# Regrouping the score blocks and the attends of a two-layer graph network into clusters, with one rotation of eight PSUM banks

## The chip, the cores and the metric

The kernel runs on one core of a Trainium2 chip. The metric is the device time of one launch in microseconds (us); lower is better. Three runs of the kernel before gave 2311.16, 2311.50 and 2311.74 us, a median of 2311.5 us. One more execution was taken with the hardware profiler; all durations below come from it.

The engines are called PE (TensorE, matrix products), ACT (ScalarE), DVE (VectorE), POOL (GpSimd) and SP (SyncE, which here only issues DMAs). Each works through its own list of instructions in order and waits on semaphores where it needs another engine's result.

## The reference

All data are float32: x is 64 x 256 x 512, adj is 64 x 256 x 256 with ones and zeros.

```python
# layer 0
feat_proj = feats @ fc_w.T + fc_b
logits = q + swapaxes(k, 2, 1)              # q, k: feat_proj times one row of weights each
masked = logits + (1.0 - adj_mat) * NEG_INF
masked = where(masked >= 0, masked, 0.01 * masked)
x1 = softmax(masked) @ feat_proj + feats
# layer 1: 8 heads of 64
Q, K, V = x1 @ W_q + b_q, x1 @ W_k + b_k, x1 @ W_v + b_v
scores = Q @ K.T / sqrt(64) + a[:, :, None] + c[:, None, :] + log(adj + 1e-9)
out = softmax(scores) @ V + x1
```

## The kernel before, in words

The 64 graphs are taken in 32 groups of two. One **step** of the program works on several groups at once: on group f the end of layer 0 and the projections of layer 1, on group a (one older) its attention, on group d (two older) the rest of its output, and on group n (one newer) the loading and the weights of layer 0. The function `step` (L1107) and `attention_and_layer_0` (L1068) write out by hand the order in which the pieces are issued: `A("scores:0")` issues `scores(0)` of group a, `F("pf.p1")` piece p1 of the product pf of group f, and so on. That order, cut to what belongs to one engine, is the order of each engine. No scheduler changes it.

**Products.** The four 512 x 512 x 512 products of a group (pf: features of layer 0; pq, pk, pv: queries, keys, values) are Strassen-like: seven block products p1 to p7 of four matmuls each. A float32 matmul is two passes of PE, so a block product shows as eight records. Three PSUM banks are reused within a product: r takes p1, then p6, p5 and p3 are added onto it; r2 takes p7, then p4 is added. Between these additions others read the same bank: `keep` (L437) lets ACT copy r after p1, p6 and p5 to SBUF, and `sum` (L442) lets DVE add such a copy to r1 or r2 and write one quarter of the result (`sum_11` reads r2 between p7 and p4). An addition onto a bank must wait for the reader before it.

**Attention of group a.** Index u is 0 to 3: graph u // 2, head group u % 2. `scores(u)` (L847) computes two blocks, jc = 0 and 1; each is four matmuls with 64 rows (two heads side by side in the rows of PE, `par`, each into a bank of its own), and one ACT exp over the pair of banks, 128 x 1024. `factor(u, jc)` (L876, DVE) multiplies by the adjacency, `both(u)` (L884, DVE) adds the two blocks, `parts(u)` (L908, DVE: a transpose and a reduction) prepares the sums of the softmax, `totals` (L922, PE) adds them over partitions. `attend(gr)` (L888) multiplies by v for one graph: 16 matmuls of 64 columns, two side by side, then two ACT copies. `turn(gr)`, `divide(gr)`, `complete(gr)` (DVE) and `store(gr)` finish a graph.

PE thus works in three shapes: full (128 rows, 128 columns), 64 rows by 128 columns (scores) and 128 rows by 64 columns (attend, totals).

**Order within a step before.** The head: pv.p5 of the step before, scores 0, attend 1 (of group d), scores 1, pv.p3, pv.p4, then the mix of layer 0 (`y`, four groups of eight records) and pf.p1, p2, p6, p7, p5, p3. The middle: scores 2, attend 0, totals, scores 3, pf.p4. Then pq, pk and pv up to p5, with scores no more. On DVE the tail of the step is: four `keys` (dot products with x), pq.sum_00, a piece of xsum, pq.sum_11, `divide:0`, four `dot_q` (on the x of group n), pq.sum_10, `complete:0`, `parts:2`, pk.sum_11, `adjt`, pk.sum_00, two `dot_k`, pk.sum_10, two `dot_k`, `turn_residual:0`, `weights:0`, `weights:1`, pv.sum_00. The x of group n goes into the only buffer of that name, so its DMA (`load_x`, L541, issued by SP) starts when `keys` has read the old x.

**PSUM.** Four single banks (`ps`) and two pairs of banks (`psc`); scores, and pq.p7 with `scores = True`, use the pairs.

Of the kernel before, what the change touches and what calls it, by code (L numbers as in the profile page):

```python
# [10 lines left out]
F32 = mybir.dt.float32  # L11
# [6 lines left out]
P = 128  # L18
# [7 lines left out]
def kernel(  # L26
# [137 lines left out]
    def fast():  # L164
        main = ExitStack()
        with main:
# [4 lines left out]
            six = main.enter_context(tc.tile_pool(name="six", bufs=6))  # L171
            ps = main.enter_context(
                tc.tile_pool(name="ps", bufs=4, space=bass.MemoryType.PSUM)
            )
            psc = main.enter_context(
                tc.tile_pool(name="psc", bufs=2, space=bass.MemoryType.PSUM)
# [4 lines left out]

            def pair(name):
                return psc.tile([P, 2, 512], F32, tag="pair", name=name)
# [205 lines left out]
            class Product:  # L389
# [5 lines left out]
                scores = False  # L395

# [21 lines left out]
                def fresh(self, n, scores=False):  # L418
                    name = f"{self.name}_{n}"
                    dst = (pair(name)[:, 0] if scores else bank(name)).rearrange(  # L420
                        "p (m k) -> p m k", m=2
                    )
                    self.add(n, dst, True)
                    return dst
# [36 lines left out]
                def p7(self):  # L461
                    self.r2 = self.fresh(7, self.scores)
# [66 lines left out]
            class Group:  # L529
# [235 lines left out]
                def begin(self):  # L765

                    g = self.g

                    def to(dst):
                        return lambda o, k: block(dst, o, k)  # L770

                    def to_v(o, k):
                        return self.v[:, TPG * k : TPG * (k + 1), o * HALF : (o + 1) * HALF]


                    self.d = {}
# [8 lines left out]
                    self.pq.scores = True  # L785
                    self.pk = Product(f"pk_{g}", "k", b, to(self.kT), False)
# [60 lines left out]
                def scores(self, u):  # L847


                    g, (gr, hg) = self.g, divmod(u, 2)  # L850
                    if u == 0:
                        self.e, self.esum, self.oTs, self.sms1, self.osb = {}, {}, {}, {}, {}
                    for jc in range(TPG):
                        t = gr * TPG + jc
                        sc = pair(f"sc_{g}_{u}_{jc}").rearrange("p a (b i) -> p a b i", b=2)
                        for pr in range(2):
                            for par in range(2):
                                rows = slice(par * HD, (par + 1) * HD)
                                nc.tensor.matmul(  # L859
                                    sc[:, par, pr, :],  # L860
                                    lhsT=self.kT[rows, 2 * hg + pr, ts(t, P)],
                                    rhs=self.qT[rows, 2 * hg + pr, ts(gr, N)],
                                    start=True,
                                    stop=True,
                                )
                        if g == NG - 1 and u == 3:

                            if jc == 0:
                                last = one.tile([P, 2, 2, 2, N], F32, tag="x", name="e_last")
                            e = last[:, jc]  # L870
                        else:
                            e = six.tile([P, 2, 2, N], F32, tag="e", name=f"e_{g}_{u}_{jc}")
                        nc.scalar.activation(e, sc, AF.Exp, bias=self.c[:, t : t + 1], scale=SCALE)  # L873
                        self.e[u, jc] = e
# [9 lines left out]
                def both(self, u):  # L884
                    self.esum[u] = two.tile([P, 2, 2, N], F32, tag="es", name=f"es_{self.g}_{u}")
                    nc.vector.tensor_tensor(self.esum[u], self.e[u, 0], self.e[u, 1], ALU.add)  # L886
# [21 lines left out]
                def parts(self, u):  # L908
# [5 lines left out]
                    pool, tag = ((two, "osb"), (one, "e0"), (one, "e0"), (one, "adj"))[u]  # L914
                    turned = pool.tile([P, NC * N], F32, tag=tag, name=f"est_{g}_{u}")
# [6 lines left out]
                def totals(self, gr, dst):  # L922


                    half = NC * N // B // 2
                    for par in range(2):
                        nc.tensor.matmul(  # L927
                            dst[par * HD : (par + 1) * HD, :].rearrange("p (a m) -> p a m", a=2),
                            lhsT=every[:, 0:HD], rhs=self.part[:, :, par * half : (par + 1) * half],
                            start=True, stop=True, skip_group_check=True,  # L930
                        )
                    self.tot = dst

                def totals_1(self):
                    self.totals(1, bank(f"tot_{self.g}_1")[:, 0 : NC * N // B])

                def totals_0(self):
                    self.totals(0, bank(f"tot_{self.g}_0")[:, 0 : NC * N // B])

                def ratios(self, gr):  # L940
                    self.rs = recip1[:, self.g % NR, gr]
                    nc.vector.reciprocal(self.rs.rearrange("p m b -> p (m b)"), self.tot)

                def ratios_of_all(self):


                    self.rs = recip1[:, self.g % NR, 1]
# [39 lines left out]
                def turn(self, gr):  # L987

                    g = self.g
                    self.osb[gr] = two.tile([P, NC * N], F32, tag="osb", name=f"osb_{g}_{gr}")  # L990
# [27 lines left out]
                def complete(self, gr):  # L1018
                    nc.vector.tensor_tensor(self.osb[gr], self.osb[gr], self.xb[gr], ALU.add)
# [5 lines left out]
                def finish(self, gr):  # L1025
# [3 lines left out]
                    self.osb[gr] = two.tile([P, NC * N], F32, tag="osb", name=f"osb_{g}_{gr}")  # L1029
# [77 lines left out]
            def step(d, a, f, n, check):  # L1107
# [24 lines left out]
                A("factor:3:0 factor:3:1 both:3")  # L1132
# [18 lines left out]
                if n is None:  # L1151
                    A("attend:1 totals_1 ratios:1 turn:1 divide:1 complete:1 store:1")
                    F("residual:1 turn_residual:1")

                    F("pv.p2 scores:0 pv.p6 pv.sum_00 factor:0:0 factor:0:1 scores:1 both:0 pv.p7")
                    F("factor:1:0 factor:1:1 both:1 scores:2 pv.p5 sums_1:0 scores:3 pv.sum_11")
                    F("ratios_t:0 ratios_r:0 factor:2:0 factor:2:1 pv.p3 pv.p4 factor:3:0 pv.sum_10")
                    F("factor:3:1 attend:0 finish:0 sums_of_e:1 attend:1")
# [8 lines left out]
                F("pv.sum_00")  # L1167
                A("parts:3")
# [237 lines left out]
```

## Time and profile before

| what | value |
|---|---|
| median of three runs | 2311.5 us |
| span of the profiled execution | 2308.8 us |
| mean granted clock of PE in that execution | 0.997 |
| busy in the span: DVE | 2124.2 us (92%) |
| busy in the span: ACT | 1071.8 us (46%) |
| busy in the span: POOL | 121.9 us (5%) |
| one step of the middle of the run, from the first y to the next | 70.88 us |
| in such a step: PE, DVE, ACT busy | 70.88, 65.9, 33.4 us |

The span runs from the first to the last instruction that the profiler recorded; the runs' time is 2.7 us longer than the span at the median, which is what lies around it. The steps repeat: of 30 distances between the starts of `y` in successive steps 29 are 70.88 us and one is 70.95 us. So one step stands for nearly all of the time, and a change per step counts some 30 times.

In the time lines below each row gives the start in us, the time in us from the first record's start to the last one's end, the engine, the line of the program, the operation, output and inputs, shapes, and the number of records that were merged. What stands in square brackets is idle time of that engine just before, and what ended it. Records of PE overlap by about 0.16 us, since a matmul's end is later than the start of its successor; for PE the distance between starts is the time that a group takes.

### The profile page before, as it was taken

The numbers are of one execution on the slowest core, as the hardware profiler recorded it, in microseconds if no ns is written. First come the engines' busy times: TensorE is split into PE (matmuls) and PEld (weight loads), VectorE is DVE, ScalarE is ACT, GpSimd is POOL, SyncE is SP. The second block draws the span as 40 slices with busy tenths as digits, with TensorE's granted clock in tenths as the row PEclk, the third lists the DMA queues.
The fourth block names the chain that finished last, engine by engine and source line by source line (L and its number), as shares of the span: only waits on it lengthen the run. The fifth ranks groups of instructions, "written<-read, shape, count | busy, mean of one in ns | idle before, by whom it ended". The sixth has DMA issues, their size and how long they took to land.

```text
span 2308.8 us, 33613 instructions
## 1 busy us (share of the span) xinstructions
PE 2294.2 (99%) x12618; PEld 1905.2 (83%) x12618; DVE 2124.2 (92%) x3180; ACT 1071.8 (46%) x1865; POOL 121.9 (5%) x120
## 2 busy tenths in 40 slices
PE   9999999999999999999999999999999999999997
PEld 6888888888888888888888888888888888888885
DVE  6899999999999999999999999999999999999997
ACT  3544444454445444454444454444544445444443
POOL 0000000000000000000000000000000000000000
PEclk9999999999999999999999999999999999999999
DMA  4122332223322233232233232332222323223312
GB/s 133 46 61 73 78 76 66 70 61 85 79 73 61 61 78 78 74 68 61 69 78 83 60 75 63 79 78 74 64 60 74 78 73 70 65 64 81 84 46 38
DMA packets 517264, 163.84 MB, mean 71 GB/s; under 512 B 415188, under 2 KB 478696, under 8 KB 517096
## 3 DMA queue, kind: packets, MB, share of 16 engines
q1 hardware_dynamic: 514440, 160.32, 28.8%
q8 instruction: 102, 1.67, 0.3%
q10 hardware_dynamic: 2656, 1.31, 0.2%
q14 instruction: 66, 0.54, 0.1%
HBM read 95.43 MB, written 66.12 MB: 70 GB/s over the span
## 4 chain that ended last, share of the span: by engine, by line
PE 98%; DVE 1%; DMA 0%; ACT 0%; issue 0%; ACTq 0%; DVEq 0%
PE pv L412 17%; PE pq L412 17%; PE pf L412 16%; PE pk L412 16%; PE sc L859 11%; PE oT L899 10%; PE y L689 9%; PE fp L718 1%; DMA fc_nat<-in_L_gnn_fc_w_dram 0%; PE rc L637 0%; DVE osb L1034 0%; PE tot L927 0%; DVE osb L1040 0%; PE xTp L705 0%; DVE osb L1033 0%; DVE x L756 0%
## 5 line engine op out<-in xcount | busy, mean ns | idle before, releaser
L873 ACT ACTIVATE e<-sc,c 128x1024 f32<-128x1024 f32 x254 | 269.0, 1110 | 79.2 <-PE sc L859 77.6
L879 DVE TENSOR_TENSOR e<-e,am 128x1024 f32<-128x1024 f32 x254 | 297.7, 1213 | 0.4 <-ACT e L873 0.4
L859 PE MATMUL sc<-qT,kT 64*128 64x256 f32 x2048 | 255.8, 390 | 0.3 <-ACT e L873 0.3
L899 PE MATMUL oT<-e,v 128*64 128x256 f32 x2032 | 233.4, 382 | 0.0
L859 PEld LDWEIGHTS sc<-qT,kT 64*128 64x128 f32 x2048 | 187.3, 187 | 52.6 <-issue 32.7
L495 POOL TENSOR_TENSOR pf_s<-pf_s,x 128x512 f32<-128x512 f32 x93 | 118.4, 1273 | 2106.1 <-ACT pf_s L494 2038.8
L689 PE MATMUL y<-e,x 128*128 128x256 f32 x992 | 225.6, 381 | 0.0
L899 PEld LDWEIGHTS oT<-e,v 128*64 128x64 f32 x2032 | 140.2, 137 | 85.3 <-issue 10.7
L689 PEld LDWEIGHTS y<-e,x 128*128 128x128 f32 x992 | 186.4, 190 | 23.7
L432 ACT ACTIVATE pq_s<-pq,cols 128x256 f32<-128x256 f32 x192 | 80.5, 470 | 249.1 <-PE pq L412 249.1
L494 ACT ACTIVATE pf_s<-pf,recip 128x256 f32<-128x256 f32 x186 | 77.9, 470 | 197.6 <-PE pf L412 197.6
L917 DVE TENSOR_REDUCE part<-est 128x32 f32<-128x1024 f32 x124 | 151.3, 1220 | 4.3
L916 DVE STREAM_TRANSPOSE est<-es 128x1024 f32<-128x1024 f32 x124 | 152.2, 1227 | 0.0
L886 DVE TENSOR_TENSOR es<-e,e 128x1024 f32<-128x1024 f32 x126 | 149.3, 1205 | 1.1
L695 ACT COPY yT<-y 128x512 f32<-128x512 f32 x124 | 72.6, 585 | 131.7 <-PE y L689 130.9
L429 ACT COPY pk_s<-pk 128x512 f32<-128x512 f32 x96 | 56.3, 586 | 165.7 <-PE pk L412 159.0
L906 ACT COPY oTs<-oT 128x512 f32<-128x512 f32 x128 | 75.0, 586 | 118.0 <-PE oT L899 97.3
L412 PE MATMUL pk<-t1b,wk 128*128 128x256 f32 x512 | 121.1, 380 | 0.4 <-DVE kT L443 0.4
L412 PE MATMUL pv<-wv,t1b_c 128*128 128x256 f32 x512 | 121.1, 380 | 0.0
L412 PE MATMUL pv<-wv,t1b 128*128 128x256 f32 x512 | 121.0, 380 | 0.0
L412 PE MATMUL pq<-x1T,wq 128*128 128x256 f32 x512 | 121.0, 379 | 0.0
L412 PE MATMUL pk<-x1T,wk 128*128 128x256 f32 x512 | 121.0, 379 | 0.0
(181 smaller groups left out, 4506.3 us busy)
## 6 DMA issues: line engine op xcount, KB each, us to landing
x<-in_x_dram SPq DMA_DIRECT2D x32, 1024.0 KB, 5.1
out_dram<-osb SPq DMA_DIRECT2D x254, 128.0 KB, 3.1
xd<-xt SPq DMA_DIRECT2D x124, 256.0 KB, 2.0
x1T<-xd SPq DMA_DIRECT2D x496, 64.0 KB, 1.9
adj<-in_adj_dram SPq DMA_DIRECT2D x128, 128.0 KB, 3.5
qrow<-q SPq DMA_DIRECT2D x31, 256.0 KB, 3.9
fc_nat<-in_L_gnn_fc_w_dram ACTq DMA_DIRECT2D x4, 256.0 KB, 3.8
wq<-in_L_gnn_W_q_dram SPq DMA_DIRECT2D x1, 1024.0 KB
```

The costliest lines, as they stand in the source:

```text
L412: nc.tensor.matmul(o, lhsT=lk[:, ts(m, P)] if len(lk.shape) == 2 else lk[:, m], rhs=rk, start=(start and m == 0 and k == 0), stop=(m == 1 ...
L432: nc.scalar.activation(dst[:, m], src[:, m], AF.Identity, bias=self.bias[:, 2 * o + m : 2 * o + m + 1],)
L494: nc.scalar.mul(s[:, m], src[:, m], self.recip[:, TPG * k + m : TPG * k + m + 1])
L495: nc.gpsimd.tensor_tensor(s, s, self.out(o, k), ALU.add)
L689: nc.tensor.matmul(y[:, ts(gr, N)], lhsT=self.x[:, gr * TPG + j, ts(c, P)], rhs=self.e0[:, j, gr, :], start=(gr == 0 and j == 0), stop=(gr ...
L859: nc.tensor.matmul(sc[:, par, pr, :], lhsT=self.kT[rows, 2 * hg + pr, ts(t, P)], rhs=self.qT[rows, 2 * hg + pr, ts(gr, N)], start=True, st ...
L873: nc.scalar.activation(e, sc, AF.Exp, bias=self.c[:, t : t + 1], scale=SCALE)
L879: nc.vector.tensor_tensor(ef, ef, self.am[:, jc, u // 2, :].unsqueeze(1).to_broadcast([P, 4, N]), ALU.mult,)
L886: nc.vector.tensor_tensor(self.esum[u], self.e[u, 0], self.e[u, 1], ALU.add)
L899: nc.tensor.matmul(oT[par * HD : (par + 1) * HD, pr, :], lhsT=self.v[:, gr * TPG + jc, ts(h, HD)], rhs=self.e[2 * gr + hg, jc][:, par, pr, :],
L916: nc.vector.transpose(turned, self.esum[u].rearrange("p a b i -> p (a b i)"))
L917: nc.vector.tensor_reduce(self.part[:, hg, :], turned.rearrange("p (m c) -> p m c", c=B), AX.X, ALU.add,)
```

## The change

The change rewrites the hand-written order and the buffers that it needs:

- all eight score blocks of a group stand together at the step's head, behind pv.p3 and pv.p4 (which move ahead of them, directly behind pv.p5 and pv.sum_00);
- each block has two single banks in place of a pair, and two ACT exps of 128 x 512 in place of one of 128 x 1024; there is one pool of eight single banks for everything, and eight e tiles in place of six;
- both attends of group a stand together in the middle, behind pf.p3 (attend 1 was at the head of the next step);
- all eight factors follow each other on DVE at the head; `both:0` and `parts:0` go ahead of pf.add_01, `both:1`, `turn:0` and `parts:1` behind pf.sum_01, `ratios:0`, `both:2` and `parts:2` behind xsum, and `turn:1`, `both:3` and `parts:3` behind `complete:0`, that is ahead of pk.sum_11;
- `totals` becomes one full matmul, moved behind pk.p1; `ratios` two reciprocals of 64 partitions each;
- some SBUF tiles that had two buffers have one (es, osb), and `complete` writes into xb.

```diff
             ps = main.enter_context(
-                tc.tile_pool(name="ps", bufs=4, space=bass.MemoryType.PSUM)
-            )
-            psc = main.enter_context(
-                tc.tile_pool(name="psc", bufs=2, space=bass.MemoryType.PSUM)
+                tc.tile_pool(name="ps", bufs=8, space=bass.MemoryType.PSUM)
             )
...
-                        sc = pair(f"sc_{g}_{u}_{jc}").rearrange("p a (b i) -> p a b i", b=2)
+                        sc = [
+                            bank(f"sc_{g}_{u}_{jc}_{par}").rearrange("p (b i) -> p b i", b=2)
+                            for par in range(2)
+                        ]
...
-                            e = six.tile([P, 2, 2, N], F32, tag="e", name=f"e_{g}_{u}_{jc}")
-                        nc.scalar.activation(e, sc, AF.Exp, bias=self.c[:, t : t + 1], scale=SCALE)
+                        e = eight.tile([P, 2, 2, N], F32, tag="e", name=f"e_{g}_{u}_{jc}")
+                        for par in range(2):
+                            nc.scalar.activation(
+                                e[:, par], sc[par], AF.Exp, bias=self.c[:, t : t + 1], scale=SCALE
+                            )
...
-                def totals(self, gr, dst):
...
+                def totals(self, gr):
+
+                    nb = NC * N // B
+                    self.all_sums = bank(f"tot_{self.g}_{gr}")[:, 0 : 2 * nb]
+                    nc.tensor.matmul(
+                        self.all_sums, lhsT=every, rhs=self.part_all[:, 0 : 2 * nb],
+                        start=True, stop=True,
+                    )
...
-                A("scores:0")
-                D("attend:1")
-                F("add_tiles")
-                A("scores:1 factor:0:0 factor:0:1 pv.sum_11 pv.p3 pv.p4")
-                D("turn:1")
-                F("parts_0")
-                A("factor:1:0 factor:1:1 pv.sum_10 both:0 both:1")
-                F("mix:0 mix:1 ysum:0 recip")
-                D("ratios_of_all divide:1 complete:1 store:1")
-                A("residual:1")
-                F("mix:2 mix:3 ysum:1 ysum:2 ysum:3")
-                A("parts:0")
-                F("pf.p1 pf.keep_1 pf.p2 pf.p6 pf.sum_00 begin send:0:0 fetch:0:0")
-                A("turn_residual:1 parts:1")
-                F("pf.p7 pf.p5 pf.p3 pf.add_01 pf.sum_11 send:1:1")
-                A("scores:2 attend:0 totals_0")
-                F("pf.sum_01 send:0:1 fetch:1:1 fetch:0:1")
-                F("copy:0")
-                A("factor:2:0 factor:2:1 scores:3 turn:0 ratios:0 both:2")
-                F("pf.p4 pf.sum_10 send:1:0 fetch:1:0")
-                F("pq.p1 pq.keep_1 pk.p1 pk.keep_1 pv.p1 pv.keep_1")
+                A("scores:0 scores:1 scores:2 scores:3")
+                F("add_tiles parts_0")
+                A("factor:0:0 factor:0:1 factor:1:0 factor:1:1")
+                A("factor:2:0 factor:2:1 factor:3:0 factor:3:1")
+                F("mix:0 mix:1 recip mix:2 mix:3 ysum:0")
+                D("ratios:1 divide:1")
+                A("residual:1")
+                F("ysum:1")
+                D("complete:1 store:1")
+                F("ysum:2 pf.p1 pf.keep_1 pf.p2 pf.p6 pf.sum_00 begin send:0:0 fetch:0:0 ysum:3")
+                A("turn_residual:1 both:0 parts:0")
+                F("pf.p7 pf.p5 pf.p3 pf.add_01 pf.sum_11 send:1:1")
+                A("attend:0")
+                F("pf.sum_01 send:0:1 fetch:1:1 fetch:0:1")
+                A("both:1 turn:0 attend:1 parts:1")
+                F("copy:0 pf.p4 pf.sum_10 send:1:0 fetch:1:0")
+                F("pq.p1 pq.keep_1 pk.p1")
+                A("totals:0")
+                F("pk.keep_1 pv.p1 pv.keep_1")
...
-                A("factor:3:0 factor:3:1 both:3")
+                A("ratios:0 both:2 parts:2")
...
-                A("complete:0 store:0 parts:2")
-                if n is None:
-                    A("parts:3")
+                A("complete:0 store:0 turn:1 both:3 parts:3")
...
-                F("pv.sum_00")
-                A("parts:3")
+                F("pv.sum_00 pv.p3 pv.sum_11 pv.p4 pv.sum_10")
```

The last step (no newer group) is rewritten in the same way: its four separate scores become one cluster behind pv.p6 and pv.sum_00.

More of the change, by code (lines that the diff above doesn't have):

```diff
@@ L170, in fast @@
             four = main.enter_context(tc.tile_pool(name="four", bufs=4))
-            six = main.enter_context(tc.tile_pool(name="six", bufs=6))
+            eight = main.enter_context(tc.tile_pool(name="eight", bufs=8))
             ps = main.enter_context(
-                tc.tile_pool(name="ps", bufs=4, space=bass.MemoryType.PSUM)
-            )
-            psc = main.enter_context(
-                tc.tile_pool(name="psc", bufs=2, space=bass.MemoryType.PSUM)
+                tc.tile_pool(name="ps", bufs=8, space=bass.MemoryType.PSUM)
             )
@@ L180, in bank @@
                 return ps.tile([P, 512], F32, tag="bank", name=name)
-            def pair(name):
-                return psc.tile([P, 2, 512], F32, tag="pair", name=name)
             dram = main.enter_context(
@@ L389, in fast @@
             class Product:
-                scores = False
                 def __init__(self, name, a, b, out, rows, bias=None):
@@ L416, in add, with fresh @@
                             )
[L418 to L422, printed above, removed]
+                def fresh(self, n):
+                    dst = bank(f"{self.name}_{n}").rearrange("p (m k) -> p m k", m=2)
                     self.add(n, dst, True)
@@ L461, in p7 @@
                 def p7(self):
-                    self.r2 = self.fresh(7, self.scores)
+                    self.r2 = self.fresh(7)
                 def p5(self):
@@ L784, in begin @@
                     self.pq = Product(f"pq_{g}", "q", b, to(self.qT), False, bq_col)
-                    self.pq.scores = True
                     self.pk = Product(f"pk_{g}", "k", b, to(self.kT), False)
@@ L859, in scores @@
                                 nc.tensor.matmul(
-                                    sc[:, par, pr, :],
+                                    sc[par][:, pr, :],
                                     lhsT=self.kT[rows, 2 * hg + pr, ts(t, P)],
@@ L865, in scores @@
                                 )
[L866 to L871, printed above, removed]
-                            e = six.tile([P, 2, 2, N], F32, tag="e", name=f"e_{g}_{u}_{jc}")
-                        nc.scalar.activation(e, sc, AF.Exp, bias=self.c[:, t : t + 1], scale=SCALE)
+                        e = eight.tile([P, 2, 2, N], F32, tag="e", name=f"e_{g}_{u}_{jc}")
[3 more added lines that the diff above has]
+                            )
                         self.e[u, jc] = e
@@ L884, in both @@
                 def both(self, u):
-                    self.esum[u] = two.tile([P, 2, 2, N], F32, tag="es", name=f"es_{self.g}_{u}")
+                    tag = "adj" if self.g == NG - 1 and u == 1 else "es"
+                    self.esum[u] = one.tile([P, 2, 2, N], F32, tag=tag, name=f"es_{self.g}_{u}")
                     nc.vector.tensor_tensor(self.esum[u], self.e[u, 0], self.e[u, 1], ALU.add)
@@ L913, in parts @@
                         self.part = self.part_all[:, 0 : 2 * nb].rearrange("p (a m) -> p a m", a=2)
-                    pool, tag = ((two, "osb"), (one, "e0"), (one, "e0"), (one, "adj"))[u]
-                    turned = pool.tile([P, NC * N], F32, tag=tag, name=f"est_{g}_{u}")
+                    turned = one.tile([P, NC * N], F32, tag="e0", name=f"est_{g}_{u}")
                     nc.vector.transpose(turned, self.esum[u].rearrange("p a b i -> p (a b i)"))
@@ L920, in parts @@
                     )
-                def totals(self, gr, dst):
[L925 to L938, printed above, removed]
+                def totals(self, gr):
[5 more added lines that the diff above has]
+                    )
                 def ratios(self, gr):
                     self.rs = recip1[:, self.g % NR, gr]
-                    nc.vector.reciprocal(self.rs.rearrange("p m b -> p (m b)"), self.tot)
-                def ratios_of_all(self):
-                    self.rs = recip1[:, self.g % NR, 1]
                     sums = self.all_sums.rearrange("p (a b m) -> p b a m", a=2, b=2)
@@ L989, in turn @@
                     g = self.g
-                    self.osb[gr] = two.tile([P, NC * N], F32, tag="osb", name=f"osb_{g}_{gr}")
+                    self.osb[gr] = one.tile([P, NC * N], F32, tag="osb", name=f"osb_{g}_{gr}")
                     nc.vector.transpose(self.osb[gr], self.oTs[gr].rearrange("p a i -> p (a i)"))
@@ L1018, in complete @@
                 def complete(self, gr):
-                    nc.vector.tensor_tensor(self.osb[gr], self.osb[gr], self.xb[gr], ALU.add)
+                    nc.vector.tensor_tensor(self.xb[gr], self.osb[gr], self.xb[gr], ALU.add)
+                    self.osb[gr] = self.xb[gr]
                 def ratios_t(self, gr):
@@ L1028, in finish @@
                     g, nb = self.g, N // B
-                    self.osb[gr] = two.tile([P, NC * N], F32, tag="osb", name=f"osb_{g}_{gr}")
+                    self.osb[gr] = one.tile(
+                        [P, NC * N], F32, tag=("osb", "e0")[gr], name=f"osb_{g}_{gr}"
+                    )
                     for hg in range(2):
@@ L1151, in step @@
                 if n is None:
-                    A("attend:1 totals_1 ratios:1 turn:1 divide:1 complete:1 store:1")
+                    A("totals:1 ratios:1 divide:1 complete:1 store:1")
                     F("residual:1 turn_residual:1")
[L1155 to L1158, printed above, removed]
+                    F("pv.p2 pv.p6 pv.sum_00 scores:0 scores:1 scores:2 scores:3")
+                    F("pv.p7 factor:0:0 factor:0:1 factor:1:0 factor:1:1 both:0 both:1")
+                    F("pv.p5 pv.sum_11 pv.p3 sums_1:0 pv.p4 pv.sum_10")
+                    F("factor:2:0 factor:2:1 ratios_t:0 ratios_r:0 factor:3:0 factor:3:1")
+                    F("attend:0 finish:0 sums_of_e:1 attend:1")
                     F("ratios_t:1 ratios_r:1 finish:1")
```

## The prediction

> **What bounds the kernel now.** I read the shares of busy time first, then the chain of waits that ended last, then the time lines of PE and DVE over one step.
>
> ```profile
> PE 2294.2 (99%) x12618; PEld 1905.2 (83%) x12618; DVE 2124.2 (92%) x3180; ACT 1071.8 (46%) x1865; POOL 121.9 (5%) x120
> ...
> PE 98%; DVE 1%; DMA 0%; ACT 0%; issue 0%; ACTq 0%; DVEq 0%
> ```
>
> PE is the bound: 98% of the chain, no stop in a step. So time falls only if PE gets less to do, and rises by every wait that PE gets. PE rows of a step's head, middle and tail:
>
> ```profile
> 1276.34 1.89 PE L412 MATMUL pv<-wv,t1b 128*128 128x256 f32 x8
> 1278.16 2.00 PE L859 MATMUL sc<-qT,kT 64*128 64x256 f32 x16
> 1280.09 3.67 PE L899 MATMUL oT<-e,v 128*64 128x256 f32 x32
> 1283.69 2.00 PE L859 MATMUL sc<-qT,kT 64*128 64x256 f32 x16
> 1285.62 2.00 PE L412 MATMUL pv<-v_s,t1b_c 128*128 128x256 f32 x8
> ...
> 1289.17 3.62 PE L689 MATMUL y<-e,x 128*128 128x256 f32 x16
> ...
> 1304.94 1.89 PE L412 MATMUL pf<-fc_s,yT 128*128 128x256 f32 x8
> ...
> 1316.14 1.89 PE L412 MATMUL pq<-x1T,wq 128*128 128x256 f32 x8
> ...
> 1340.31 1.89 PE L412 MATMUL pk<-t1b,wk 128*128 128x256 f32 x8
> ...
> 1347.22 1.89 PE L412 MATMUL pv<-wv,t1b 128*128 128x256 f32 x8
> ```
>
> The last four are pf.p3, pq.p1 (I call its start Q), pk.p4 at Q+24.17 and pv.p5. DVE and ACT around that tail:
>
> ```profile
> 1326.32 0.08 DVE L519 DVE_READ_ACCUMULATOR2_ANT c<- 128x1 f32 x1
> ...
> 1331.80 0.69 DVE L519 CUSTOM_DVE_ANT_0 jq<-x,wq_row 128x512 f32<-128x512 f32 x1 [0.69 <-DMA x<-in_x_dram]
> ...
> 1338.77 0.68 DVE L443 TENSOR_TENSOR kT<-pk,pk_s 128x512 f32<-128x512 f32 x1
> ...
> 1349.57 0.68 DVE L443 TENSOR_TENSOR v<-pv,pv_s 128x512 f32<-128x512 f32 x1
> ...
> 1349.14 0.59 ACT L429 COPY pv_s<-pv 128x512 f32<-128x512 f32 x1 [0.67 <-PE pv L412]
> ...
> 2262.30 1.99 PE L412 MATMUL pk<-t1b,wk 128*128 128x256 f32 x8 [0.42 <-DVE kT L443]
> ```
>
> These are: the end of keys (Q+10.26), dot_q held up by the DMA of x, pk.sum_11, pv.sum_00, the copy of pv.p5, and pk.p4 of the last step, where parts:2 and parts:3 both stand ahead of pk.sum_11. That row is the one to remember: pk.p4 adds onto the bank that pk.sum_11 reads, so late DVE work stops PE. In the ordinary step pk.sum_11 ends at Q+23.3, only 0.86 us before PE needs it.
>
> **1. Fewer changes of shape (gain).** Pure passes take 0.216 us: 16 records of pf take 3.45 us (1296.31 to 1299.76); scores and attends take that per pair of records. From 1276.34 to 1289.17 there are 12.83 us for 56 such units (8+8+16+8+16), 12.09 us; 0.74 us is spent on four changes of shape. From 1304.94 to 1316.14: 11.20 us for 48 units, 10.36 us; 0.84 us for four more with totals. So 1.58 us a step. After, there are four changes: into and out of the cluster, 0.40 us (both kinds are in the first stretch, about 0.2 each), and full to attend and back. In the last step pv.p4 to attend costs 0.15 us; attend to full is in no row without totals between; between 0.1 and 0.2, taken as 0.20 like scores to full. Totals costs 0.21 us as a full matmul, like rc of that size among the y. Together 0.95: **gain 0.63 us** a step.
>
> **2. Does PE wait in the cluster (nothing, up to 2.3 us).** [...] ACT has 16 exps of 512 to do. A 1024 exp repeats every 1.01 us (the row of two takes 2.12, one 1.11), a 256-wide read of PSUM with bias every 0.37 (two 0.84, one 0.47); between them 512 repeats every 0.585 and takes 0.69. PE fills two banks in 0.86 us (eight records of 0.108), ACT empties two in 1.17. [...] By the rows, with the first exp 1.18 us behind the first score (1350.22 against 1349.04): block k, counted from 0, starts at 0.10+0.864k, so block 7 at 6.15; its second bank is free when exp 7 ends, 1.18+7x0.585+0.69+0.05=6.02. The first y starts at 7.11, its bank is free at 6.6. Eight banks are just lead enough, by 0.1 us. I take the rows: no wait. ACT's 1.27 us more per step (16x0.585-8x1.01) lie in its idle time, but its last exp starts at 9.96, and DVE's last factor (1.135 each, in the exps' pace) ends at 11.84.
>
> **3. DVE from the head to Q (0.95 us late).** Counted from the first score. ACT after the exps: two yT copies from 10.54, four small copies, two more yT (the last ends at 15.1, y_3 being done at 14.5), residual:1 until 16.75, the two scalings of pf.p1 until 17.6; POOL's addition (1.28) until 19.0. DVE meanwhile: recip, ysum, ratios, divide until 14.9, ysum:1 at 15.15 (it waits for that last yT), complete:1 until 16.97, ysum:2; then it waits until 19.0 for POOL. From there: pf.sum_00 0.91, send 0.64, ysum:3 0.60: 21.15. Now turn_residual:1, and here a queue counts: with one xb per graph in flight it writes the buffer that store:1 is sending off. Store:1's four DMAs are issued by SP at 0, 0.65, 1.36 and 2.10 us behind complete:1, and the landing of one takes 3.1 us at the median, 2.5 at best; in the step of 1297 the packets end 4.4 us behind complete. So 21.6: DVE waits about 0.5 (bounds 0.4 and 1.1). Then turn_residual 1.12, both 1.14, parts 2.40, add_01 0.78, sum_11 0.90, send 0.64, sum_01 0.86, send 0.64, both 1.14, turn 1.17, parts 2.41: 34.85. PE reaches Q at 33.7 (cluster 7.11, y and rc 7.24, six pf products 10.36, both attends 7.05, p4 with its change of shape 1.93), and pf.sum_10 could start at Q+0.2. DVE is **0.95 us late** (bounds 0 and 2).
>
> PE itself doesn't feel this yet: pq.p6 needs xsum:1, which ends at Q+4.2, at Q+5.4; pq.p2 needs the last piece of x1T, some 6.9 us behind the start of pf.sum_10, Q+8.0, at Q+8.8. ACT's copies of attend 1 wait for turn:0 (there is one oTs), until about 33.2, copy:0 then ends at 34.9; pv.p1 needs it at Q+3.7.
>
> **4. DVE from Q to pk.p4 (loss).** Up to the end of keys two factors go (2.39) and two reciprocals (0.73) and a parts (2.40) come: +0.74, so keys end at Q+0.95+11.00. The x of the next group waits for that, with nothing ahead of it on SP; dot_q started 5.40 us behind keys (other steps 5.2 to 6.4): Q+17.35. pq.sum_00 to divide:0 fit in between, as before. From dot_q to pk.sum_11 it was 6.97 us; turn:1 (1.16) and both:3 (1.14) come, parts:3 takes the place of parts:2: 9.27. So pk.sum_11 starts at Q+26.62, takes 0.68, and PE goes on 0.05 later (in the last step 2262.30 against DVE's end at 2262.25): Q+27.35. PE is there at Q+24.17+0.21=24.38. **Wait 2.97 us**, and 0.10 to get going (the first two records after such a stop stand 0.32 apart, not 0.22). Behind pk.p4 on PE stand all of pv and the cluster.
>
> **5. pv.p5, p3, p4 in a row (loss).** p3 adds onto the bank that ACT copies after p5. Before, scores and an attend lay between. The copy started 1.92 us behind p5, takes 0.59, plus 0.05: p3 can start 2.56 us behind p5, not 1.73. **Wait 0.83+0.10 us**, also where DVE is early. Then p5 starts at Q+34.36, p3 at 36.92, p4 at 38.75. p4 needs pv.sum_11 too: from pk.sum_11 to pv.sum_00 10.80, then 0.60+0.68+0.05: Q+38.75, the same moment. Without waits p4 would start at Q+34.74: **4.01 us lost** a step.
>
> **Sum.** A step changes by 4.01-0.63=+3.38 us; 30 full steps: +101.4. First step: only p3's wait, +0.9. Last step: 0.6 less as elsewhere, three score clusters fewer (1.2), one attend on its own fewer (0.3), p3's wait +0.9, and the sums of the last e (L978) now wait for four factors and the ratios that DVE does only behind pv.sum_10 (0.8+4.5+1.7, against 3.6 us of attend 0), +3.4: +2.2. The profiled execution: 2308.8+104.5=2413.3 us. The median of the runs shown is 2.7 us above the span: **2416 us**.
>
> **Rivals.**
> - *The shapes decide (faster).* DVE has 5 us free in each step (65.9 of 70.88 busy) and ACT half its time. If that slack lay where the new work goes, only the gain stays: 30x0.63 and some 2 at the end, 2291 us. It decides if PE's waits of a step total under 0.63 us. Against it: the slack lies ahead of sum_10, sum_11 and dot_q, where DVE waits for PE, ACT and x, and the tail from dot_q on has none.
> - *Only the copy between p5 and p3.* DVE makes pk.sum_11 in time: 0.93-0.63=+0.30 a step, about 2323 us. It needs DVE 3 us earlier at that place than I count.
> - *The cluster at ACT's pace too.* If a bank comes free late (pv's last two are among the eight), PE loses up to 2.3 us at the head; about half of it falls into time that DVE's chain loses anyhow: about 2455 us. For it: the lead of 0.1 us.
> - That the order isn't as written is out: in the built program the scores' matmuls all follow pv.p4, and the attends each other.
>
> **Chances.** Main case 0.73, 2365 to 2450: lateness -29 to +31, x -6 to +20, exp pace up to 0.63 +20, not all at one end. Shapes decide 0.09; copy only 0.10; ACT's pace 0.08. The range is 2355 to 2455. No change within 0.2%, which is about what a measurement of this kernel can tell, lies between the first two rivals: 0.03. Faster 0.08, slower 0.89.
>
> **What would show it.** pk.p4 idle 3 us on DVE kT in each step; pv.p3 idle 0.8 us on ACT pv_s; a step of 74.3 us; hardly any idle time of sc on ACT; turn_residual idle on the DMA of out. It is wrong if pk.p4 follows pk.p3 without a gap, or if the steps are under 70.88 us.

## Result, and the profile after

| kernel | median | range | profiled span | granted clock of PE | mean step |
|---|---|---|---|---|---|
| before | 2311.62 us (4 runs) | 2311.16 to 2313.27 | 2308.8 us | 0.997 | 70.88 us |
| changed | 2490.02 us (4 runs) | 2486.49 to 2494.12 | 2489.4 us | 0.983 | 76.64 us |

The changed kernel takes 1.0769 times as long, 95% interval 1.0754 to 1.0785: it is slower by 178 us, where the forecast had 104 us and a range that ended at 2455 us. The direction was right and the size was not.

The page of the changed kernel, first the busy times, then the two rows of the chain of waits by engine and by group that matter:

```profile
PE 2338.5 (94%) x12554; PEld 1924.0 (77%) x12554; DVE 2155.1 (87%) x3212; ACT 1086.1 (44%) x2121; POOL 130.4 (5%) x120
...
PE 45%; DVE 34%; DMA 12%; issue 3%; SPq 3%; ACT 1%; DVEq 0%; POOL 0%; ACTq 0%; POOLq 0%
...
L404 PE MATMUL pk<-t1b,wk 128*128 128x256 f32 x512 | 147.2, 438 | 92.7 <-DVE kT L432 92.7
L850 PE MATMUL sc<-qT,kT 64*128 64x256 f32 x2048 | 230.7, 380 | 0.0
```

PE's share of the chain fell from 98% to 45%; DVE and the DMAs hold the rest. The group row of pk has what the forecast named: 92.7 us of idle time behind DVE's kT. But it holds a second thing: a record of pk takes 438 ns at the mean, one of the scores 380. The scores have no idle time, as forecast. The list of waits (total, times, longest, in us), PE first, then DVE:

```profile
PE pk L404 <- DVE kT L432: 92.7, 31, 3.6
PE pv L404 <- ACT pv_s L418: 21.6, 32, 0.7
...
DVE jq L508 <- DMA x<-in_x_dram: 47.8, 30, 2.2
DVE xb L832 <- DMA out_dram<-xb: 44.1, 31, 5.0
```

The first two are the two forecast waits, at 3.07 and 0.68 us of idle time for each full step. This idle time counts from the end of PE's last record, which overlaps the next by 0.16 us; from start to start pk.p4 comes 3.24 us late and pv.p3 0.84 us. One step of PE's time line, from pq.p1 (Q) on:

```profile
1263.66 1.89 PE L404 MATMUL pq<-x1T,wq 128*128 128x256 f32 x8
...
1286.64 1.89 PE L404 MATMUL pk<-x1T,k_s 128*128 128x256 f32 x8
1292.04 2.41 PE L404 MATMUL pk<-t1b,wk 128*128 128x256 f32 x8 [3.51 <-DVE kT L432]
1294.24 3.20 PE L404 MATMUL pv<-wv,t1b_c 128*128 128x256 f32 x8
...
1303.30 1.99 PE L404 MATMUL pv<-v_s,t1b_c 128*128 128x256 f32 x8 [0.68 <-ACT pv_s L418]
1305.13 1.89 PE L404 MATMUL pv<-wv,t1b 128*128 128x256 f32 x8
1306.95 7.18 PE L850 MATMUL sc<-qT,kT 64*128 64x256 f32 x64
1314.06 3.72 PE L678 MATMUL y<-e,x 128*128 128x256 f32 x16
```

pk.p4 starts at 1292.04, after 3.51 us of idle time. Then the pace changes: pk.p4 and the product behind it take 2.20 and 3.04 us from start to start, where eight records take 1.73 everywhere else. The busy times by stretch show why (the length of the stretch, the busy times of PE, PEld, DVE, ACT and POOL, then PEclk, the granted clock, the DMA share and GB/s); the first row is the stop, the second pk.p4 and what follows:

```profile
1288.50:1292.00 3.50, 0.03 (x1) 0.00 (x0) 3.43 (x5) 1.45 (x4) 0.00 (x0) 1.00 1.15 196
1292.00:1297.30 5.30, 5.26 (x17) 4.34 (x18) 5.23 (x12) 3.24 (x3) 0.00 (x0) 0.68 0.47 71
1297.30:1303.30 6.00, 5.33 (x25) 4.36 (x23) 5.44 (x9) 1.85 (x4) 0.00 (x0) 1.00 0.23 36
```

PE runs at a mean of 0.68 behind the stop: for part of the stretch its records stand 0.432 us apart, twice the usual 0.216. That is half clock, and the forecast had no term for it.

The distances between PE's records, summed over the 30 full steps and compared with the kernel before, give the step's account:

| us per step | forecast | measured |
|---|---|---|
| pk.p4 waits for pk.sum_11, with getting going | 3.07 | 3.34 |
| pv.p3 waits for ACT's copy, with getting going | 0.93 | 0.94 |
| records at half clock behind pk.p4's stop | 0 | 1.05 |
| pq.p6, pq.p2, pq.p3 and totals late | 0 | 0.98 |
| changes of shape (what remains) | -0.63 | -0.55 |
| sum | 3.38 | 5.76 |

Thirty steps at 5.76 us are 172.7 of the 180.6 us between the two spans. The other 7.9 us lie in what comes before the first of these steps and behind the last, where the forecast had 3.1; they were not traced further.

### The profile page after: what moved, and what is told of

Read it like the earlier page. It is cut to its first block, busy times and chain, and to the rows that moved or that the text cites. A ratio compares the mean times of both kernels' runs of the same rounds, so it can differ in the third digit from the quotient of the medians.

```text
span 2489.4 us, 33742 instructions
## 1 busy us (share of the span) xinstructions
PE 2338.5 (94%) x12554; PEld 1924.0 (77%) x12554; DVE 2155.1 (87%) x3212; ACT 1086.1 (44%) x2121; POOL 130.4 (5%) x120
## 4 chain that ended last, share of the span: by engine, by line
PE 45%; DVE 34%; DMA 12%; issue 3%; SPq 3%; ACT 1%; DVEq 0%; POOL 0%; ACTq 0%; POOLq 0%
PE pv L404 11%; PE y L678 9%; PE sc L850 9%; PE pf L404 7%; DMA x<-in_x_dram 7%; DVE est L904 4%; DVE es L875 4%; DVE jq L508 3%; PE pk L404 3%; DVE part L905 3%; DVE x L490 2%; PE pq L404 2%; SPq L793 2%; DMA xd<-xt 2%; PE oT L888 2%
## 5 line engine op out<-in xcount | busy, mean ns | idle before, releaser
L859 ACT ACTIVATE e<-sc,c 128x512 f32<-128x512 f32 x512 | 299.3, 735 | 69.9 <-PE sc L850 69.9
L484 POOL TENSOR_TENSOR pf_s<-pf_s,x 128x512 f32<-128x512 f32 x93 | 126.9, 1364 | 2274.8 <-ACT pf_s L483 2217.5
L404 PE MATMUL pk<-t1b,wk 128*128 128x256 f32 x512 | 147.2, 438 | 92.7 <-DVE kT L432 92.7
L850 PE MATMUL sc<-qT,kT 64*128 64x256 f32 x2048 | 230.7, 380 | 0.0
L850 PEld LDWEIGHTS sc<-qT,kT 64*128 64x128 f32 x2048 | 196.1, 187 | 32.4 <-issue 10.6
L404 PEld LDWEIGHTS pk<-t1b,wk 128*128 128x128 f32 x512 | 108.7, 218 | 121.8 <-DVE kT L432 105.2
L432 DVE TENSOR_TENSOR v<-pv,pv_s 128x512 f32<-128x512 f32 x96 | 64.1, 687 | 89.7 <-PE pv L404 84.9
L508 DVE CUSTOM_DVE_ANT_0 jq<-x,wq_row 128x512 f32<-128x512 f32 x128 | 88.5, 692 | 51.1 <-DMA x<-in_x_dram 47.8
L404 PE MATMUL pv<-wv,t1b_c 128*128 128x256 f32 x512 | 131.8, 403 | 0.0
L818 ACT ACTIVATE xv<-x1T,cols 128x256 f32<-128x256 f32 x256 | 109.1, 498 | 50.1 <-DVE osb L966 46.2
```

The lines of the kernel that those rows point to most:

```text
L404: nc.tensor.matmul(o, lhsT=lk[:, ts(m, P)] if len(lk.shape) == 2 else lk[:, m], rhs=rk, start=(start and m == 0 and k == 0), stop=(m == 1 ...
L484: nc.gpsimd.tensor_tensor(s, s, self.out(o, k), ALU.add)
L508: nc.vector.tensor_tensor_reduce(out=junk, in0=src, in1=w_row, scale=1.0, scalar=init, op0=ALU.mult, op1=ALU.add, accum_out=dst,)
L818: nc.scalar.activation(self.xv[:, c].rearrange("p (t a m) -> p t a m", t=TPG, m=B), self.x1T[:, c // 2, gr].rearrange("p (a t c m) -> p c ...
L850: nc.tensor.matmul(sc[par][:, pr, :], lhsT=self.kT[rows, 2 * hg + pr, ts(t, P)], rhs=self.qT[rows, 2 * hg + pr, ts(gr, N)], start=True, st ...
L859: nc.scalar.activation(e[:, par], sc[par], AF.Exp, bias=self.c[:, t : t + 1], scale=SCALE)
```

## The experiments

**Theory A**: PE loses the time at two waits that DVE's and ACT's order causes, plus the half clock that was measured behind pk.p4's stop (0.432 us per record), plus late pieces of pq; the cluster itself is harmless. **Theory B**, in several forms: the loss is a property of the new layout (eight shared banks, exps of 512, clusters on PE), or of the amount of DVE work, so that it only moves when the order is changed.

### 1. Is the half clock a cost of its own?

Between pk.p3 and pk.p4, ten more records of PE (five matmuls into a bank that nobody reads):

```diff
-                F("pk.p3 pk.p4 pk.sum_10")
+                F("pk.p3")
+                if a is not None and n is not None:
+                    F("filler:5")
+                F("pk.p4 pk.sum_10")
```

> The kernel after, with five full matmuls of 256 columns (2.2 us) into a bank that nobody reads, put between pk.p3 and pk.p4 in the 30 full steps, so that PE works through most of the wait for pk.sum_11. Theory A [...]: no half-clock window after pk.p4, a mean granted clock above 0.99, and about 2445 us in place of 2490, although PE does more. Theory B (the clock is not what costs time; the loss over the forecast comes from DVE and DMA waits): 2485 to 2495 us, or slower by what the filler delays.

Measured: 2460.3 us, 1.0645 times the kernel before, with the 95% interval [1.0627, 1.0663]. PE does 2.16 us more per step and the kernel is 30 us *faster* than the changed one. In its time line, around pk.p4:

```profile
1275.06 2.32 PE L996 MATMUL fill<-wk 128*128 128x256 f32 x10
1278.68 1.99 PE L404 MATMUL pk<-t1b,wk 128*128 128x256 f32 x8 [1.30 <-DVE kT L432]
```

and the busy times of the stretches ahead of pk.p4 and behind it:

```profile
1273.30:1278.68 5.38, 4.08 (x19) 3.24 (x19) 5.31 (x6) 2.17 (x5) 0.00 (x0) 1.00 0.61 126
1278.68:1284.00 5.32, 5.32 (x25) 4.70 (x26) 5.25 (x12) 3.24 (x3) 0.00 (x0) 1.00 0.67 108
```

pk.p4 comes no earlier: filler and remaining wait together are as long as the stop was (3.3 us per step). But the granted clock is 1.00 behind it, and no record of the full steps stands 0.43 us from the next; there were about 130 such in the changed kernel. The step is 0.99 us shorter, which is the half-clock term. So the stop and the half clock behind it are two costs, and the second can be had back alone.

### 2. ACT's copy between pv.p5 and pv.p3

```diff
-                F("pv.p2 pv.p6")
+                F("pv.p6 pv.p2")
...
-                F("pv.p7 pv.p5")
+                F("pv.p5 pv.p7")
```

> The kernel after, with pv in the order p6 p2 p5 p7 p3 p4, so that p7 lies between p5 and p3, and ACT's copy of p5 is hidden. Theory A (DVE's tail up to pv.sum_11 ends only shortly ahead of pv.p4, so removing p3's wait of 0.7 us gains at most that): 2468 to 2488 us, with pv.p3 no longer idle. Theory B (the copy is the main loss, as the other waits follow from it): 2460 us or less.

Measured: 2481.0 us, 1.0735 [1.0717, 1.0752]. The wait for ACT fell from 21.6 to 6.5 us in all. In the profiled execution, which was the fastest of the four (2472.6 us, the others some 2481), the step gained 0.58 us of the 0.94: the half clock took some back (1.3 us per step there, granted clock 0.980), and in 11 of the steps p3 still waits for ACT. So a wait that is taken away need not be gained in full.

### 3. The DVE work ahead of pk.sum_11, added to the kernel before

One of the moved pieces alone, in the kernel before: `parts:3` (2.40 us by the forecast) ahead of pk.sum_11 in every step, with its scratch tile in the buffer of `parts:2`.

```diff
-                A("complete:0 store:0 parts:2")
-                if n is None:
-                    A("parts:3")
+                A("complete:0 store:0 parts:2 parts:3")
...
-                A("parts:3")
```

> The kernel before, with one piece moved alone: parts:3 (2.4 us of DVE) ahead of pk.sum_11 in place of behind pv.sum_00 (its scratch tile in e0). Theory A (DVE has only 0.86 us in hand at pk.sum_11): pk.p4 idle about 1.5 us a step on DVE kT, no half clock [...], +1.65 us x 30: about 2361 us. Theory B (DVE's 5 us of idle time per step take it up): 2310 to 2315 us.

Measured: 2366.8 us, 1.0243 [1.0226, 1.026]; PE's first wait:

```profile
PE pk L412 <- DVE kT L443: 46.6, 31, 2.9
```

That is 1.53 us of idle time in a full step; from start to start pk.p4 comes 1.70 us late, against 2.40 - 0.86 = 1.54 from the lead that the forecast read out of the time line before. With 0.10 us to get going, that accounts for 1.80 of the 1.86 us by which the step grew; the granted clock is 0.998. So step 4's mechanism holds, without clusters, eight banks or attends, and its way of counting is 0.16 us short here.

### 4. Keys earlier: is the x of the next group the lock?

The changed kernel with `keys` and `load_x` ahead of `ratios:0 both:2 parts:2`, so that the DMA of x starts sooner:

```diff
-                A("ratios:0 both:2 parts:2")
                 F("keys:2 keys:3 keys:0 keys:1")
                 X("load_x")
+                A("ratios:0 both:2 parts:2")
```

> The kernel after, with keys and load_x ahead of ratios:0, both:2 and parts:2 (4.3 us of DVE), which then lie in the wait for x. Theory A (the chain keys, x, dot_q, pk.sum_11 sets pk.p4): dot_q comes about 2.4 us earlier, pk.p4's wait falls below 1 us, no half clock, about 2375 us (2355 to 2405). Theory B (the tail's work on DVE decides whenever it starts, because DVE is late from the head on): pk.p4 still idle over 2 us, 2450 us or more.

Measured: 2414.45 us, 1.0443 [1.0425, 1.046]: 75.6 us better than the changed kernel, but short of A's 2375. pk.p4's wait halves (43.5 us in all, 1.43 per step) and does not go. DVE no longer waits for x at all (47.8 us in the changed kernel), and nothing but its own work stands between dot_q and pk.sum_11 any more: the x of the next group held up about half of the wait, DVE's own lateness the rest. Half clock nearly goes too (granted clock 0.994, 0.983 in the changed kernel): it follows 4 of the stops at pk.p4, which are at most 2.3 us long here, in place of 18.

### 5. The tail's new work moved to the next head

`both:3 parts:3` behind pv.sum_10 in place of ahead of pk.sum_11:

```diff
-                A("complete:0 store:0 turn:1 both:3 parts:3")
+                A("complete:0 store:0 turn:1")
+                if n is None:
+                    A("both:3 parts:3")
...
+                A("both:3 parts:3")
```

> The kernel after, with both:3 and parts:3 (3.55 us of DVE) taken out of the tail and put behind pv.sum_10, at the head (scratch tile in adj). Theory A (DVE has too little slack for its new order as a whole: work taken from one side of the chain shows on the other): pk.p4 no longer waits, but ysum comes some 3 us later, so that PE waits at pf.p6 or at pq.p6 instead, and p3's wait of 0.8 us stays: 2340 to 2420 us. Theory B (only the work ahead of pk.sum_11 is in the wrong place): all waits but p3's go, about 2320 us.

Measured: 2490.56 us, 1.0777 [1.0756, 1.0799]. Both figures missed; the time is that of the changed kernel. pk.p4's wait is gone (0.5 us in all), and the list of waits has this in its place:

```profile
PE pf L404 <- DVE tb L344: 60.8, 30, 2.0
PE pv L404 <- ACT pv_s L418: 29.8, 32, 1.9
```

pf's second input, the sums of y, stands on DVE behind the eight factors, and the factors now stand behind `both:3 parts:3`. The lateness appears at the head of the step instead of at its tail, with half-clock stretches of its own (some 0.9 us per step at that product, granted clock 0.986). The expectation counted what left the tail and not what the head has no room for.

### 6. Eight single banks and exps of 512, alone

The kernel before, in its own order, with one pool of eight banks and two exps per block:

```diff
-                tc.tile_pool(name="ps", bufs=4, space=bass.MemoryType.PSUM)
-            )
-            psc = main.enter_context(
-                tc.tile_pool(name="psc", bufs=2, space=bass.MemoryType.PSUM)
+                tc.tile_pool(name="ps", bufs=8, space=bass.MemoryType.PSUM)
...
-                        nc.scalar.activation(e, sc, AF.Exp, bias=self.c[:, t : t + 1], scale=SCALE)
+                        for par in range(2):
+                            nc.scalar.activation(
+                                e[:, par], sc[par], AF.Exp, bias=self.c[:, t : t + 1], scale=SCALE
+                            )
```

> The kernel before, its order untouched, with one pool of eight single banks and two exps of 512 per block in place of one of 1024 (16 x 0.585 against 8 x 1.01 us on ACT). Theory A (this part is hidden by ACT's idle time): 2308 to 2316 us. Theory B (the longer exps or the shared rotation hold PE up): 2325 us or more, with sc or y idle on ACT.

Measured: 2310.43 us, 0.9999 [0.999, 1.0008]. The banks and the 256 additional exps cost nothing in that order. B's form "the layout" falls.

### 7. Two clusters of four, DVE's order nearly as before

The kernel of experiment 6 with scores 0 and 1 together ahead of attend 1, and scores 2 and 3 together ahead of attend 0:

```diff
-                A("scores:0")
+                A("scores:0 scores:1")
...
-                A("scores:1 factor:0:0 factor:0:1 pv.sum_11 pv.p3 pv.p4")
+                A("factor:0:0 factor:0:1 pv.sum_11 pv.p3 pv.p4")
...
-                A("scores:2 attend:0 totals_0")
+                A("scores:2 scores:3 attend:0 totals_0")
...
-                A("factor:2:0 factor:2:1 scores:3 turn:0 ratios:0 both:2")
+                A("factor:2:0 factor:2:1 turn:0 ratios:0 both:2")
```

> The same kernel with eight banks and the order of before, but scores 0 and 1 together ahead of attend 1, and scores 2 and 3 together ahead of attend 0; nothing on DVE moves. Theory A (each change of PE's shape costs 0.15 to 0.2 us and nothing else is touched): two changes of shape fewer per step, -0.4 us x 30, about 2300 us, faster than before. Theory B (a cluster makes PE wait for exps or e tiles): sc or oT idle on ACT, 2312 us or more.

Measured: 2384.66 us, 1.0316 [1.0299, 1.0334]: a miss.

```profile
PE sc L856 <- DVE x L495: 18.3, 30, 0.6
PE pq L406 <- DMA x1T<-xd: 15.1, 24, 1.6
```

The scores lose 1.76 us per step, 1.25 of it in the middle cluster. That cluster takes banks in rotation, and its third block comes to those of pf, which DVE's sums of x still have to read; x1T, which is made from the same sums, comes late too. What holds the head's cluster up by the other 0.50 us was not traced. So a cluster was not free of itself here: the middle one stood where the banks that it takes were not read yet.

### 8 to 10. The clusters kept, the order of DVE and ACT rewritten

The changed kernel's clusters and banks, with DVE's pieces put where their readers need them. Its main lines:

```diff
-                A("turn_residual:1 both:0 parts:0")
+                A("both:0")
+                F("pf.sum_00 begin send:0:0 fetch:0:0 ysum:3")
+                A("parts:0 turn_residual:1")
...
-                A("ratios:0 both:2 parts:2")
                 F("keys:2 keys:3 keys:0 keys:1")
                 X("load_x")
+                A("ratios:0 both:2 parts:2")
...
-                A("complete:0 store:0 turn:1 both:3 parts:3")
-                F("pk.p7 pk.p5 pk.sum_11 residual:0")
+                A("complete:0 store:0 turn:1")
+                F("pk.p7 pk.p5 pk.sum_11")
+                A("both:3 parts:3")
+                F("residual:0")
...
+                F("pv.p6 pv.p2 pv.p5 pv.p7 pv.sum_00 pv.sum_11")
                 X("weights:0")
+                F("pv.p3 pv.p4")
                 X("weights:1")
+                F("pv.sum_10")
```

> The kernel after with its clusters, but another order on DVE: both:0 ahead of pf.sum_00, turn_residual:1 behind parts:0, keys ahead of ratios:0, both:2 and parts:2, pk.sum_11 ahead of both:3 and parts:3, pv in the order p6 p2 p5 p7 with pv.sum_00 and sum_11 ahead of the weights. Theory A (the clusters' gain of 0.63 us a step is real and only DVE's order costs): hardly any wait at pk.p4 and pv.p3, no half clock, 2290 to 2330 us. Theory B (DVE, with some 67 of 70 us busy, cannot be fitted to the clusters in any such order): waits of 1 us or more in other places, 2340 us or more.

Measured: 2367.54 us, 1.0247 [1.023, 1.0265]. The waits of pk, pq and pv.p3 are gone, but for one of 0.5 us at pq, and one is left in each step, at pv.p5. PE's row in the time line:

```profile
1378.84 1.99 PE L404 MATMUL pv<-wv,t1b 128*128 128x256 f32 x8 [1.37 <-ACT pv_s L418]
```

and the two rows of ACT's that explain it:

```profile
1377.19 1.13 ACT L564 ACTIVATE am<-am,eps 128x1024 f32<-128x1024 f32 x1
...
1378.22 0.56 ACT L418 COPY pv_s<-pv 128x512 f32<-128x512 f32 x1
```

ACT does `add_eps` first and the copy of pv.p6 next, and PE waits for the copy. So in the next kernel `mask add_eps` goes behind pv.p2, `weights:0` ahead of pv.sum_00 and pv.sum_11, and `turn_residual:0` to the step's end:

```diff
-                F("turn_residual:0")
                 if n is None:
+                    F("turn_residual:0")
...
-                X("mask add_eps")
-                F("pv.p6 pv.p2 pv.p5 pv.p7 pv.sum_00 pv.sum_11")
+                F("pv.p6 pv.p2")
+                X("mask add_eps")
+                F("pv.p5 pv.p7")
                 X("weights:0")
-                F("pv.p3 pv.p4")
+                F("pv.sum_00 pv.sum_11 pv.p3 pv.p4")
                 X("weights:1")
-                F("pv.sum_10")
+                F("pv.sum_10 turn_residual:0")
```

> The reordered version, with ACT's mask and add_eps put behind the copy of pv.p6 (so that pv.p5 finds its copy), the exp of weights:1 issued ahead of the last sums, and turn_residual:0 last. Theory A (the clusters' gain of 0.63 us of PE time per step is there to be had, and only the order of DVE and ACT gave it away): pv.p5's wait (1.43 us per step) and the lag at the scores (0.5) go, period about 70.3 us, time 2290 to 2305 us, faster than before by 0.3 to 0.9%. Rival B (with eight banks and both attends together DVE has no place for the step's sums; the wait turns up at another piece): not below 2312 us, with an idle time of 0.6 us or more per step at one PE row that was free of it in the run before.

Measured: 2300.42 us (2299.97 to 2302.84, 5 runs), 0.9948 [0.9934, 0.9961]. It is faster than both kernels, 0.5% faster than the one before. The busy times of its page:

```profile
PE 2279.1 (99%) x12554; PEld 1910.5 (83%) x12554; DVE 2175.9 (95%) x3212; ACT 1084.7 (47%) x2121; POOL 131.1 (6%) x120
```

and PE's time line of one step, from pk.p3 to the y:

```profile
1264.97 1.89 PE L404 MATMUL pk<-x1T,k_s 128*128 128x256 f32 x8
1266.69 1.89 PE L404 MATMUL pk<-t1b,wk 128*128 128x256 f32 x8
...
1277.52 1.99 PE L404 MATMUL pv<-wv,t1b 128*128 128x256 f32 x8 [0.30 <-DVE v L432]
1279.44 7.18 PE L850 MATMUL sc<-qT,kT 64*128 64x256 f32 x64
1286.55 3.72 PE L678 MATMUL y<-e,x 128*128 128x256 f32 x16
```

pk.p4 follows pk.p3 at 1.72 us, without a gap, with the same clusters, banks, exps and attends as in the changed kernel, and with no less work for DVE (2175.9 us busy against 2155.1). So Theory B's other forms fall too. The 0.30 us ahead of pv.p4 stands in one step only. The mean step is 70.40 us, 0.48 less than before, and 21 of the 30 steps take 70.26 us, 0.62 less: the gain from fewer changes of shape, kept at last. DVE is busy for 95% of the span, so there is little room left in this order. How little, the last run tells; it differs in one piece, `turn_residual:0` (a transpose of 1.25 us on DVE), back where it was:

```diff
+                F("turn_residual:0")
                 if n is None:
-                    F("turn_residual:0")
...
-                F("pv.sum_10 turn_residual:0")
+                F("pv.sum_10")
```

> As the run before it, but turn_residual:0 (0.66 us of DVE at most per tile) stays ahead of the sums of v. Theory A: its place matters only where DVE is late at pv's sums: the exp of weights:1 is done a little later, so the scores lag by some 0.3 us per step, time 2295 to 2320 us. Rival B: no difference from the run before it beyond 2 us, or a new idle time above 0.6 us per step in both.

Measured: 2331.4 us, 1.008 [1.0067, 1.0094], 31 us more than without it.

```profile
PE pv L404 <- DVE v L432: 23.9, 30, 1.4
```

The size was under-counted: one DVE instruction of 1.25 us in the wrong place costs 0.99 us of every step, at pv.p4, which waits for pv.sum_11, and not at the scores, where it was expected.

## Why the forecast was right and wrong

**Shapes (step 1): right.** About 0.55 us of 0.63 in the changed kernel, and 0.62 in the steps of experiment 9 in which nothing waits.

**No wait in the cluster (step 2): right.** The 64 records of the scores stand in 7.11 us, with no idle time. ACT's row bears out the pace of 0.585 us per exp, 299.3 us for 512:

```profile
L859 ACT ACTIVATE e<-sc,c 128x512 f32<-128x512 f32 x512 | 299.3, 735 | 69.9 <-PE sc L850 69.9
```

So the 2.3 us that step 2 had as its upper bound, 16 exps at 0.585 us (9.4 us) against 7.1 us of scores, did not come: eight banks were enough of a lead for this cluster. The lead is thin all the same. In experiment 8, where the first exp came 1.8 us behind the first score in place of 1.18, the cluster lost 0.52 us.

**DVE's lateness at Q (step 3): too small.** pf.sum_10 was to start at Q+1.15 and turn_residual:1 to wait 0.5 us. In the step with Q at 1340.64, from DVE's time line:

```profile
1328.95 1.25 DVE L832 STREAM_TRANSPOSE xb<-xv 128x1024 f32<-128x1024 f32 x1 [0.97 <-DMA out_dram<-xb]
...
1342.21 0.87 DVE L490 SCALAR_TENSOR_TENSOR x<-pf,recip,pf_s 128x256 f32<-128x256 f32 x2
...
1345.52 0.69 DVE L369 TENSOR_TENSOR t1b<-x1T 128x512 f32<-128x512 f32 x1 [1.70 <-DMA x1T<-xd]
...
1359.94 0.69 DVE L508 CUSTOM_DVE_ANT_0 jq<-x,wq_row 128x512 f32<-128x512 f32 x1 [0.51 <-DMA x<-in_x_dram]
1369.41 0.68 DVE L432 TENSOR_TENSOR kT<-pk,pk_s 128x512 f32<-128x512 f32 x1
```

The store's wait is 0.97 us there (44.1 us over 31 times, 1.3 at the mean without the longest, where the forecast had 1.1 as the upper bound), pf.sum_10 starts at Q+1.57, and DVE then waits 1.70 us for a piece of x1T, which pf's late sums had sent late; this is the longest of seven such waits. **"PE itself doesn't feel this yet" failed**: I set each piece's own arrival against its reader, and left out that DVE stands idle in front of the first. pq.p6, pq.p2, pq.p3 and totals lose 0.98 us per step at the mean, from nothing to 3.1 us in single steps. That this comes from the order of DVE's and ACT's work is shown by experiment 9, where 0.10 us is left with the same clusters on PE; which of its moves removed the rest was not tried one by one, and what makes it so uneven stays open.

**pk.p4's wait (step 4): right in mechanism, right in size by compensation.** keys ended at Q+14.11 (forecast Q+11.95) and dot_q began at Q+19.30 (Q+17.35), 2 us late; dot_q to pk.sum_11 took 9.47 us (9.27). PE was late by then as well, through pq, so pk.p4 came 3.24 us late from start to start, next to 2.97: two errors that nearly cancelled. Experiment 3 confirms the mechanism on its own.

**pv.p3's wait (step 5): right**, 0.94 against 0.93; experiment 2 takes most of it away.

**The sum failed at a term that wasn't in it.** A stop of 3 us was charged as 3 us. PE is at half clock after 18 of the 30 stops at pk.p4, which costs 1.05 us more per step, and experiment 1 shows it as a cost of its own. With the 0.98 us of the late pq, these two terms are 61 of the 74 us by which the forecast fell short; without them its own terms come to 3.34 + 0.94 - 0.55 = 3.73 us per step, some 2427 us.

The length of a stop does not tell whether half clock follows. In the changed kernel's trace the 18 stops that were followed by it show 2.20 to 3.55 us of idle time, the 12 that were not 2.37 to 3.56 us. It lasted 3.41 us behind sixteen of them and 6.83 us behind two. The shortest stop, of 2.20 us, and the longest, of 3.56 us:

```profile
2286.76:2290.17 3.41, 1.21 (x7) 0.73 (x5) 3.34 (x5) 1.33 (x3) 0.00 (x0) 1.00 1.14 197
2290.17:2293.59 3.42, 3.42 (x9) 2.71 (x10) 2.99 (x6) 2.36 (x3) 0.00 (x0) 0.50 0.43 63
...
2051.24:2054.65 3.41, 1.63 (x8) 1.10 (x6) 3.34 (x4) 2.17 (x5) 0.00 (x0) 1.00 0.69 119
2054.65:2058.07 3.42, 1.64 (x8) 1.46 (x9) 3.42 (x5) 0.51 (x1) 0.00 (x0) 1.00 0.75 111
2058.07:2061.48 3.41, 3.41 (x17) 3.02 (x16) 3.34 (x9) 2.74 (x3) 0.00 (x0) 1.00 0.76 120
```

In the 3.41 us up to the end of the shorter stop PE works for 1.21 us, and for the next 3.42 us it is at half clock. Around the longer stop PE works for 1.63 us in one row and 1.64 us in the next, and the clock stays at 1.00 in the row behind. What decides between followed and not followed is left open here.

An estimate from the changed kernel's figures: at half clock a record takes 0.432 us in place of 0.216, so 3.41 us of it cost at most 1.71 us. Sixteen times 3.41 and twice 6.83 us, 68.3 us, cost at most 34.1 us, 1.14 us for each of 30 steps, beside the 1.05 us measured; some 1.1 us per step belonged in the sum.

**The rivals.** The cluster at ACT's pace did not occur, and "only the copy" fell with pk.p4's wait, which is there in every step. "The shapes decide" (2291 us) comes near to what the clusters can give, 2300 us in experiment 9, but only after DVE's and ACT's order was rewritten around them.

## What to carry to other kernels

When pieces are gathered on one engine, the gain there is easy to count; what decides is where the work that hangs on them lands on the *other* engines' queues. For each moved piece, list what now stands behind it and how much lead its reader had: a lead of 0.86 us covered a third of one piece of 2.40 us here, and one transpose of 1.25 us made the difference between a loss and a gain. The stops of PE at pk.p4 cost more than their length here, 1.05 us per step for the half clock behind 18 of 30; where such a stop can't be removed, matmuls that keep PE busy through it can be cheaper than the stop alone (2460 against 2490 us here).

## What the runs showed of the chip that was not expected

- After 18 of 30 stops of 2.2 to 3.6 us PE was at half clock, 0.432 us per record, for 3.41 us or twice that. The length of the stop did not decide: one of 2.20 us was followed by half clock, one of 3.56 us was not.
- Ten useless records ahead of pk.p4 made the kernel 30 us faster (experiment 1).
- A wait that was removed at one place came back elsewhere with the time unchanged (experiment 5: 92.7 us gone at pk, 60.8 us new at pf, and the longer waits of pv, pq and totals).
